# Depthwise 3x3 convolutions from three row-shifted copies in blocks of 32 channels, in place of nine taps on one window

## The chip, the cores and the metric

The kernel runs on one core of a Trainium2 chip. The metric is device time in microseconds (us), the median of several runs; a profile is one further execution, recorded instruction by instruction. The engines are TensorE (PE in the profile, its weight loads PEld), VectorE (DVE), ScalarE (ACT), GpSimd (POOL) and SyncE (SP), which here issues almost all transfers between the memory of the chip (DRAM) and the buffers of the core.

## The reference

Four images of 56 x 56 positions with 96 channels pass through four layers. Layer 0 is a state-space scan in four directions with a feed-forward part; layer 1 has two depthwise convolutions and again a scan in four directions; layers 2 and 3 are linear attention with a quantised feed-forward part. The change touches the convolutions of layer 1 alone:

```python
def _dwconv3(x, w, b):
    y = jax.lax.conv_general_dilated(x, w, (1, 1), [(1, 1), (1, 1)], feature_group_count=x.shape[1], ...)
    return y + b[None, :, None, None]
...
c = jax.nn.relu(_bn(_dwconv3(xc, dw_w, dw_b), ...))        # 96 channels
c = jnp.einsum('bchw,oc->bohw', c, pw_w) + pw_b[None, :, None, None]
conv_out = jnp.transpose(_bn(c, ...), (0, 2, 3, 1))
xz = _ln(x, ln_g, ln_b) @ in_proj_w.T
xm, z = jnp.split(xz, 2, axis=-1)
xm = jax.nn.silu(_dwconv3(xm, conv_w, conv_b))             # 192 channels
...                                                        # the scan of xm in four directions -> y
fused = jnp.concatenate([conv_out, (_ln(y, ...) * silu(z)) @ out_proj_w.T], axis=-1) @ fus_w.T + fus_b
return x + _ln(fused, ...)
```

Each channel has its own 3 x 3 weights, and the image has a border of zeros.

## The kernel before

Channels lie on partitions, positions along the free dimension. An image (L = 3136 positions) is cut into NCW = 7 chunks of CW = 448 positions, which are CR = 8 rows of HS = 56. All is in float32 but for the attention layers' feed-forward part.

**The scan** (`scans`) is the backbone. Its 8 passes (two layers, four images) have 224 rounds each: 4 directions, 7 chunks, NE = 2 halves of 96 channels and NQ = 4 groups of states. In a round VectorE makes two products with `b` (line 695, `b` being a product of TensorE, line 597) and runs three scans (line 702), which need `da` from ScalarE (line 654); GpSimd makes the third product from `cb` (line 690) and multiplies the states by `cb` (line 744), and TensorE adds up the result in four blocks of 32 columns (`add_up`, line 775). `keep_busy` fills TensorE with products with zeros (line 762), as many as a number WARM = 6.8 exceeds the work planned for the round, in which a planned unit counts PER_P = 1.6. The inputs `dt`, `du` and `cb` are loaded through SP's queue by `prepare` (lines 514 and 533), one to four rounds before they are used.

**The lanes** are all the other work: generators `load`, `middle`, `fuse` and `attend`, one of each for each image. Pass p of the scan runs beside `load(1..3)` (p = 0), beside `middle(p - 1)` (p = 1 to 4), and beside `fuse(p - 5)` and `attend(p - 5)` (p = 5 to 7); `fuse(3)` and `attend(3)` begin in pass 7, a chunk as soon as its last direction is summed. What is left when the scans are done runs in `alone` after `late`, with more buffers and no pacing.

A lane runs its seven chunks through `overlap`, up to three at a time (`depth`, 2 for `convolve`, 6 after `late`). A chunk is a generator that yields a slot before each step: the letter is the half of a round ("C" or "F"), the digit the PSUM banks that it holds, `a` and `p` the planned time on ScalarE and TensorE. `room` lets a step run only if the backlog with it stays below ACT_LIMIT = 4.0 and PE_LIMIT = 7.0; `half_round` takes 0.9 and 2.4 from the backlogs twice in a round, and the scan's own work is charged to them too (line 720). The instructions of TensorE, VectorE, ScalarE and GpSimd follow this order exactly; SP issues transfers in the order of the program and stops at one whose buffer is still in use.

**The convolutions.** In `middle(i)`, layer 1's projection writes `md` to DRAM. `convolve` then loads for each chunk two windows (128 and 64 channels) of up to 10 rows with `window` (line 930) into a ring of NWIN = 3 buffers, and `conv` runs nine products with diagonal matrices (line 919), one for each tap, in three steps of three taps. The second part has 64 rows and 64 columns and is split into two halves of four rows. A tap at the image's border covers fewer rows. `diagonals` builds the matrices on GpSimd (line 901), 18 for `middle` and 9 for `fuse`, once each. In `fuse(i)` the same runs on x with 96 channels; the window is kept to the end of the chunk, where line 1162 adds its middle rows to the result. `attend` follows, with two layers of a feed-forward part (`ffn`); line 1189 runs once for each of its chunks, and line 1232 or 1242 stores the chunk.

Of the kernel before, what the change touches and what calls it, by code (L numbers as in the profile page):

```python
# [11 lines left out]
F32 = mybir.dt.float32  # L12
F16 = mybir.dt.float16
BF16 = mybir.dt.bfloat16
F8 = mybir.dt.float8e5
AF = mybir.ActivationFunctionType
ALU = mybir.AluOpType
# [3 lines left out]
HS = 56  # L21
L = HS * HS
C = 96
DI = 192
NS = 16
NE = 2
NG = 3
NQ = 4
NT = 112
CW = 448  # L30
CR = CW // HS
# [5 lines left out]
NCS = L // CS  # L37
RANK = (12, 6)
NW, LATE_NW = 13, 20
NWIN = 3  # L40
OWN = ()
OWN_TAIL = ()

# [2 lines left out]
BANKS, LATE_BANKS = 2, 4  # L46
DEPTH, LATE_DEPTH = 3, 6
# [40 lines left out]
def lay_out(i):  # L88
    i = {k: np.asarray(v) for k, v in i.items()}
    c96, c128, w96, w128, q96, q128 = Cols(C), Cols(128), Cols(C), Cols(128), Cols(C), Cols(128)  # L90
    p0, p1 = "L0_conv_", "L1_conv_"
# [3 lines left out]
    for n in (  # L95
        "dw_b bn1_g bn1_b bn1_m bn1_v pw_b bn2_g bn2_b bn2_m bn2_v ln_g ln_b fus_b fus_ln_g fus_ln_b"
    ).split():
        c96.add("1" + n, i[p1 + n][:, None])
    c96.add("1dw_w", i[p1 + "dw_w"].reshape(C, 9))
    for l in "23":  # L100
        c96.add(l + "bq", i[f"L{l}_attn_bqkv"][:C, None])
        c96.add(l + "bff", i[f"L{l}_attn_bff"][:, None])
# [14 lines left out]
    for l, (xw, dw, db, al, dd) in enumerate(scan):  # L117
        r = RANK[l]
        for k in range(4):
            t = xw[k].T  # L120
            m = np.zeros((128, NE, 2, 64), np.float32)
# [7 lines left out]
            a = al[k].reshape(NE, NG, 32, 4, NQ).transpose(3, 2, 0, 4, 1).reshape(128, -1)  # L129
# [3 lines left out]
    c128.add("0b1", i[p0 + "ffn_b1"].reshape(3, 128).T)  # L133
    for n, v in (
        ("1conv_b", i[p1 + "conv_b"][:, None]),
        ("1conv_w", i[p1 + "conv_w"].reshape(DI, 9)),
        ("1g", i[p1 + "out_norm_g"][:, None]),
        ("1b", i[p1 + "out_norm_b"][:, None]),
    ):
        c128.add(n + "a", v[:128])  # L140
        c128.add(n + "b", v[128:])
# [5 lines left out]
    f = i[p1 + "fus_w"].T  # L147
# [3 lines left out]
    w = i[p0 + "out_w"].T  # L151
# [15 lines left out]
class Net:  # L167
    def __init__(self, ctx, tc, aps, at, out):
        self.tc, self.nc, self.aps, self.at, self.out = tc, tc.nc, aps, at, out
        pool = lambda name, **kw: ctx.enter_context(tc.tile_pool(name=name, **kw))  # L170
        self.const = pool("const", bufs=1)
        self.big = pool("big", bufs=1)
        self.psum = pool("psum", bufs=1, space=bass.MemoryType.PSUM)
        self.dram = pool("dram", bufs=1, space=bass.MemoryType.DRAM)
        self.nw, self.nwin, self.depth, self.banks, self.ring = NW, NWIN, DEPTH, BANKS, None
        self.setup()
        self.dg = None
        self.kept = (0, 0, 0)
        self.ready = set()
        self.live, self.g = [], {}  # L180
        self.backlog, self.paced = [0.0, 0.0], False
        self.work, self.tables = 0.0, False
        self.both = self.big.tile([C, NE, L], F32, name="U")
        self.U = [self.both[:, e] for e in range(NE)]
        self.Y = [self.big.tile([C, L], F32, name=f"Y{e}") for e in range(NE)]
        self.wp = pool("work", bufs=2)
        self.scan_pool = ExitStack()
        self.sp = self.scan_pool.enter_context(tc.tile_pool(name="scan", bufs=2))
        self.pool = pool
        d = lambda name, *shape: [self.dram.tile(list(shape), F32, name=f"{name}{i}") for i in range(NB)]  # L190
        self.xd, self.xrd = d("x", C, L), d("xr", C, L)
        self.ud, self.zd, self.yd, self.md = d("u", DI, L), d("z", DI, L), d("y", DI, L), d("m", DI, L)

    def late(self):

        self.scan_pool.close()
        self.wp = self.pool("late", bufs=2)
        self.nw, self.nwin, self.depth, self.banks = LATE_NW, LATE_DEPTH, LATE_DEPTH, LATE_BANKS
        tags = (("ps", BANKS), ("da0", 1), ("da1", 1), ("da2", 1), ("pp", 1), ("b", 1), ("y", 1))
        self.ring = cycle([t for t in tags for _ in range(t[1])])  # L200

# [8 lines left out]
    def par(self, group, name):  # L210
        a, n = self.at[group][name]
        return self.tiles[group][:, a : a + n]
# [37 lines left out]
    def setup(self):  # L250
        nc, tc, const = self.nc, self.tc, self.const
        par = self.par
# [93 lines left out]
        with tc.tile_pool(name="stage", bufs=1) as st:  # L346
# [10 lines left out]
            self.some = self.upper(self.tiles["w128"][:, :CS])  # L357
            self.minus = const.tile([128, 64], BF16, name="minus")
            nc.vector.tensor_scalar(self.minus[64:], self.ident[64:, 64:], -1.0, None, ALU.mult)
            self.zeros = const.tile([128, C], BF16, name="zeros")  # L360
            nc.vector.memset(self.zeros, 0.0)
            t = st.tile([C, 2, 3, 128], F32, name="q96")
            nc.scalar.dma_start(t.rearrange("p l m f -> p (l m f)"), self.aps["q96"])
# [395 lines left out]

    def add_zeros(self, n):  # L760
        for _ in range(n):
            self.nc.tensor.matmul(self.y[:C], self.zeros, self.some, start=False, stop=False)  # L762

    def add_up(self, ch, e, q, hc):

# [124 lines left out]
        self.nc.sync.dma_start(t, d[:, s])  # L890
        return t

    def diagonals(self, *weights):

        t = self.wp.tile([128, 9, 192], F32, name="dg", bufs=1)
        out, n = [], 0
        for w in weights:
            p = w.shape[0]
            d = t[:p, :, n : n + p]
            for tap in range(9):  # L900
                self.nc.gpsimd.tensor_scalar_mul(d[:, tap], self.ident[:p, :p], w[:, tap : tap + 1])
                yield "F0"
            out.append(d)
            n += p
        return out

    def conv(self, diag, win, lo, *parts):

        taps = [4, 0, 1, 2, 3, 5, 6, 7, 8]
        for n, tap in enumerate(taps):
            dy, dx = tap // 3 - 1, tap % 3 - 1
            x0, x1 = max(0, -dx), min(HS, HS - dx)
            for ps, r0, rows in parts:
                o = ps.rearrange("p (a b) -> p a b", b=HS)
                a, e = max(r0, -dy), min(r0 + rows, HS - dy)
                self.nc.tensor.matmul(  # L919
                    o[:, a - r0 : e - r0, x0:x1], diag[:, tap], win[:, a + dy - lo : e + dy - lo, x0 + dx : x1 + dx],  # L920
                    start=n == 0, stop=n == 8,
                )
            if n in (2, 5):
                yield f"C1 p{3.8 / len(parts)}"

    def window(self, d, rows, c):

        lo, hi = max(0, CR * c - 1), min(HS, CR * c + CR + 1)
        t = self.wp.tile([128, CR + 2, HS], F32, name="win", bufs=self.nwin)[:rows]
        self.nc.sync.dma_start(  # L930
            t[:, : hi - lo].rearrange("p a b -> p (a b)"), d[:, lo * HS : hi * HS]
        )
        return t, lo

    def overlap(self, part, n, depth=9, ready=lambda c: True):

# [66 lines left out]
    def middle(self, i):  # L1003

        nc = self.nc
        par = self.par
        w2 = par("w128", "0w2").rearrange("p (m c) -> p m c", m=3)

# [41 lines left out]
        yield from self.overlap(part, NCW)  # L1050

        if self.dg is None:
            self.dg = yield from self.run(self.diagonals(par("c128", "1conv_wa"), par("c128", "1conv_wb")[:64]))
        dga, dgb = self.dg

        def convolve(c):
            s = slice(c * CW, (c + 1) * CW)
            wa, lo = self.window(self.md[i][:128], 128, c)
            wb, _ = self.window(self.md[i][128:], 64, c)
            yield "C0"  # L1060
            yield "C1 p3.8"
            ps = self.ps()[:, :CW]
            yield from self.conv(dga, wa, lo, (ps, c * CR, CR))
            yield "F0 a3.2"
            t = self.w()
            nc.scalar.activation(t, ps, AF.Silu, bias=par("c128", "1conv_ba"))
            self.exp_and_ln()
            yield "C1 p1.9"
            ps = self.ps()
            o = [ps[64 * h : 64 * h + 64, : CW // 2] for h in range(2)]  # L1070
            yield from self.conv(dgb, wb, lo, *[(o[h], c * CR + h * CR // 2, CR // 2) for h in range(2)])
            nc.sync.dma_start(self.ud[i][:128, s], t)
            yield "F0 a3.4"
            t = self.w(64)
            for h in range(2):
                nc.scalar.activation(
                    t[:, h * CW // 2 : (h + 1) * CW // 2], o[h], AF.Silu, bias=par("c128", "1conv_bb")[:64]
                )
            self.exp_and_ln()
            yield "C0"  # L1080
            nc.sync.dma_start(self.ud[i][128:, s], t)
# [16 lines left out]
    def fuse(self, i):  # L1098

        nc = self.nc  # L1100
        par = self.par
        if len(self.dg) > 1:
            self.dg = yield from self.run(self.diagonals(par("c96", "1dw_w")))
        (dgx,) = self.dg

        def part(c):
            s = slice(c * CW, (c + 1) * CW)
            d, z = self.yd[i], self.zd[i]
            za, zb = self.get(z[:128], 128, s), self.get(z[128:], 64, s)
            win, lo = self.window(self.xd[i], C, c)  # L1110
            yield "C0"
            yield "C1 p3.8"
            ps = self.ps()[:C, :CW]
            yield from self.conv(dgx, win, lo, (ps, c * CR, CR))
            ya, yb = self.get(d[:128], 128, s), self.get(d[128:], 64, s)
            yield "F0 a.7"
            fo = self.w(C)
# [38 lines left out]
            f = yield from self.spread_factor(1e-5, (sq, self.avg96[:, :1]))  # L1156
            yield "C1"
            nc.vector.tensor_tensor(fo, fo, f, ALU.mult)
            yield "C0"
            x = self.w(C)  # L1160
            r = c * CR - lo
            nc.gpsimd.tensor_tensor(x, fo, win[:, r : r + CR].rearrange("p a b -> p (a b)"), ALU.add)
            yield "F0 a.5"
            nc.scalar.activation(x, x, AF.Identity, bias=par("c96", "1fus_ln_b"))
            yield "C1 p1.3"
# [206 lines left out]
```

## Time and profile before

| | |
|---|---|
| median of 3 runs | 8356.53 us (8340.41 to 8364.75) |
| the profiled execution | 8364.46 us, its span 8362.7 us |
| mean granted clock of TensorE | 0.898 |
| busy: PE, DVE, POOL, ACT | 7469.6, 7516.6, 7177.3, 6109.8 us |
| weight loads of TensorE (beside its products) | 2721.6 us |
| DMA: bytes, mean rate | 1417.77 MB, 170 GB/s |
| window loads: count, KB, us to landing | 84 in all; for example 20 of 280 KB, 5.1 us |

A row of the costliest groups reads: line, engine, operation, output and inputs with their shape, count; after the first bar the busy time and the mean duration in ns of one; after the second the idle time of the engine just before them, and what ended most of it. A row of the waits reads: who waited, for what, us in total, times, longest. Busy time is summed over stages with different limits, so what counts is which wait ends last in a stage.

### The profile page before, as it was taken

The page shows a single profiled execution, that of the slowest core. Times are in us where ns is not written, and L with a number is a line of the kernel's source. Part 1 is how long each engine was busy: PE and PEld are TensorE (multiplying, and loading weights), DVE is VectorE, ACT ScalarE, POOL GpSimd, SP SyncE. Part 2 cuts the span into 40 slices and gives each one's busy share as a digit, 9 for nine tenths or more (in the row PEclk, how much of TensorE's full clock was granted, in tenths as well). Part 3 has the DMA queues.
Part 4 walks back from the last instruction along what each step waited for, and adds up shares of the span by engine and source line. Part 5 has one row for each costly group of instructions (what it writes and reads, how often), then busy time and mean ns, then how long its engine had stood idle before and what let it go on. Part 6 is the DMA issues. An engine that isn't in the chain of part 4 may idle for free. (4 is left out here: it accounts for less than half of the span.)

```text
span 8362.7 us, 119228 instructions
## 1 busy us (share of the span) xinstructions
PE 7469.6 (89%) x33633; PEld 2721.6 (33%) x33633; DVE 7516.6 (90%) x9555; ACT 6109.8 (73%) x12807; POOL 7177.3 (86%) x3991
## 2 busy tenths in 40 slices
PE   7889888898889988898899979988899888998997
PEld 3333233232333223232322323333333333333344
DVE  5999999999998999999998999999999999999921
ACT  5778878776787768786777766777776777767736
POOL 4999989989998999899898998998888888889820
PEclk8899989899999989998898989988899888999986
DMA  5777777678766777677776777676766667666721
GB/s 154 179 188 189 203 179 182 167 175 199 178 174 170 172 188 181 172 177 184 177 175 167 174 185 176 166 170 172 186 166 162 166 173 182 167 160 167 175 57 48
DMA packets 944159, 1417.77 MB, mean 170 GB/s; under 512 B 169410, under 2 KB 936644, under 8 KB 942628
## 3 DMA queue, kind: packets, MB, share of 16 engines
q1 hardware_dynamic: 942720, 1408.34, 68.2%
q8 instruction: 264, 4.33, 0.2%
q14 instruction: 403, 3.30, 0.1%
q10 hardware_dynamic: 772, 1.80, 0.1%
HBM read 1141.42 MB, written 268.14 MB: 169 GB/s over the span
## 5 line engine op out<-in xcount | busy, mean ns | idle before, releaser
L702 DVE TENSOR_TENSOR_SCAN h<-da,h 128x449 f32<-128x449 f32 (+1 forms) x5376 | 5507.1, 1071 | 134.9 <-ACT da L654 79.3
L744 POOL TENSOR_TENSOR hc<-h,cb 128x1344 f32<-128x1344 f32 x1792 | 4884.8, 2726 | 598.8 <-DVE h L702 413.6
L654 ACT ACTIVATE da<-dt,na 128x448 f32<-128x448 f32 x5376 | 3353.1, 632 | 1143.2 <-DVE h L702 1104.4
L695 DVE TENSOR_TENSOR h<-du,b 128x448 f32<-128x448 f32 x3584 | 2019.6, 604 | 182.7 <-PE b L597 112.6
L775 PE MATMUL y<-hc,four 128*32 128x448 f32 x14336 | 1913.0, 609 | 17.8 <-POOL hc L744 17.4
L690 POOL TENSOR_TENSOR h<-du,cb 128x448 f32<-128x448 f32 x1792 | 1754.1, 979 | 141.4 <-DMA cb<-cd 110.1
L762 PE MATMUL y<-w,zeros 128*96 128x448 bf16 x4843 | 1354.0, 397 | 0.0
L597 PE MATMUL b<-cf,sel 128*128 128x448 bf16 x1792 | 680.2, 380 | 631.2 <-DVE h L695 626.6
L762 PEld LDWEIGHTS <-zeros 128*96 128x96 bf16 x4843 | 603.2, 135 | 1111.0 <-issue 965.1
L775 PEld LDWEIGHTS y<-hc,four 128*32 128x32 f32 x14336 | 294.2, 113 | 1182.5 <-issue 660.5
L433 PE MATMUL pp<-U,wd 96*128 96x448 f32 x896 | 664.5, 830 | 12.1 <-DMA U<-u 8.3
L771 PE MATMUL y<-Y,ident 96*96 96x448 f32 x672 | 542.9, 898 | 18.6 <-ACT Y L782 14.3
L919 PE MATMUL ps<-win,dg 64*64 64x220 f32 (+11 forms) x1998 | 547.3, 471 | 0.0
L479 PE MATMUL pp<-cf,wd 12*96 12x448 f32 (+1 forms) x896 | 476.2, 613 | 71.7 <-ACT dtc L489 47.6
L672 ACT COPY carry<-h 128x3 f32<-128x3 f32 x1536 | 301.9, 197 | 282.3 <-DVE h L702 276.2
L504 POOL TENSOR_TENSOR duc<-dtc,U 96x896 f32<-96x896 f32 x224 | 483.1, 2157 | 3.3 <-ACT dtc L491 3.3
L782 ACT COPY Y<-y 96x448 f32<-96x448 f32 x448 | 341.7, 763 | 77.7 <-PE y L775 76.8
L919 PEld LDWEIGHTS ps<-win,dg 64*64 64x64 f32 (+2 forms) x1998 | 239.7, 162 | 321.5 <-issue 289.0
L667 ACT COPY h<-carry 128x3 f32<-128x3 f32 x1536 | 280.2, 182 | 66.3 <-POOL hc L744 63.5
L489 ACT ACTIVATE dtc<-pp,wd 96x448 f32<-96x448 f32 x448 | 281.7, 629 | 31.3 <-PE pp L479 27.4
L597 PEld LDWEIGHTS <-sel 128*128 128x128 bf16 x1792 | 183.8, 103 | 336.1 <-issue 272.7
L827 PEld LDWEIGHTS ps<-avg,w 96*112 96x112 f32 (+2 forms) x1944 | 249.9, 193 | 108.1 <-issue 59.0
(427 smaller groups left out, 5933.9 us busy)
## 6 DMA issues: line engine op xcount, KB each, us to landing
cb<-cd SPq DMA_DIRECT2D x3584, 112.0 KB, 3.9
dt<-dd SPq DMA_DIRECT2D x1792, 168.0 KB, 4.3
du<-dd SPq DMA_DIRECT2D x1792, 168.0 KB, 4.1
dd<-dtc SPq DMA_DIRECT2D x224, 336.0 KB, 3.0
dd<-duc SPq DMA_DIRECT2D x224, 336.0 KB, 3.1
U<-u SPq DMA_DIRECT2D x112, 168.0 KB, 4.7
z<-w SPq DMA_DIRECT2D x56, 224.0 KB, 4.5
u<-w SPq DMA_DIRECT2D x56, 224.0 KB, 3.9
```

What stands on the lines that cost most here:

```text
L433: self.nc.tensor.matmul(ch.ps.rearrange("p (a b) -> p a b", b=HS), ch.par.wx[:, e], self.in_order(self.U[e], ch.orient, ch.c * CS, CS), st ...
L504: self.nc.gpsimd.tensor_tensor(in_rows(ch.duc), in_rows(ch.dtc), u[:, :, lo : lo + CS // HS], ALU.mult)
L597: self.nc.tensor.matmul(ps, self.sel[:, q], self.upper(ch.cf), start=True, stop=True)
L654: nc.scalar.activation(da[g][:, INNER], ch.dt[e][:, g], AF.Exp, scale=ch.par.na[:, e, q, g : g + 1])
L690: nc.gpsimd.tensor_tensor(tokens(hs[n])[:, 2], ch.du[e][:, 2], ch.cb[q][:, 1], ALU.mult)
L695: nc.vector.tensor_tensor(tokens(hs[n])[:, g], ch.du[e][:, g], bs[n], ALU.mult)
L702: nc.vector.tensor_tensor_scan(h[:, way], da[g][:, way], h[:, way], 0.0, ALU.mult, ALU.add)
L744: nc.gpsimd.tensor_tensor(hc, tokens(hs[n]), ch.cb[q][:, 0].unsqueeze(1).to_broadcast([128, NG, CS]), ALU.mult,)
L762: self.nc.tensor.matmul(self.y[:C], self.zeros, self.some, start=False, stop=False)
L771: nc.tensor.matmul(o, w, self.in_order(a, ch.orient, ch.c * CS, CS), start=True, stop=False)
L775: nc.tensor.matmul(self.y[32 * n : 32 * n + 32], self.four, hc[:, g], start=n == 3, stop=n == 3 or q == NQ - 1,)
L919: self.nc.tensor.matmul(o[:, a - r0 : e - r0, x0:x1], diag[:, tap], win[:, a + dy - lo : e + dy - lo, x0 + dx : x1 + dx], start=n == 0, st ...
```

## The change

A window now holds three copies of the same rows, shifted by one image row: partitions 0 to 31 the row above, 32 to 63 the row itself, 64 to 95 the row below, for a block of 32 channels. A product with a matrix of 96 rows and 32 columns (three diagonals of 32, one below the other) adds up the three taps of a column of the 3 x 3 weights, so three products make a block's convolution. Two blocks share a window buffer, so 192 channels are six blocks in three buffers, 96 channels three blocks in two. The four blocks of a chunk write to four groups of 32 PSUM partitions, and the order goes over blocks within a tap column. The steps of three taps become one step.

What moves with it: the rows at the image's border need zeros, so the DRAM tensors `x` and `m` get a row of zeros at each end (`xw`, `mw`; `xd`, `md` become views of their inside), written by six transfers at the start of each `middle`. A window takes three loads instead of one, `convolve` loads its third window when it issues the first convolution, and `fuse` loads x again for the last addition in place of reading the window's middle rows. NWIN goes from 3 to 5 and late from 6 to 7. The weights are laid out by row of taps (`by_row`), and the 27 diagonals have 32 columns. The planned work of a convolution goes from three steps of 3.8 to one of 4 and, for the second part, from three of 1.9 to one of 2.

```diff
-NWIN = 3
+NWIN = 5
...
+    by_row = lambda w: w.reshape(-1, 32, 3, 3).transpose(2, 1, 0, 3).reshape(C, -1)
+    c96.add("1dw_w", by_row(i[p1 + "dw_w"]))
+    c96.add("1conv_w", by_row(i[p1 + "conv_w"]))
...
+        self.xw, self.mw = d("x", C, L + 2 * HS), d("m", DI, L + 2 * HS)
+        self.xd, self.md = [[t[:, HS : HS + L] for t in a] for a in (self.xw, self.mw)]
...
-        self.nw, self.nwin, self.depth, self.banks = LATE_NW, LATE_DEPTH, LATE_DEPTH, LATE_BANKS
+        self.nw, self.nwin, self.depth, self.banks = LATE_NW, LATE_DEPTH + 1, LATE_DEPTH, LATE_BANKS
...
-    def conv(self, diag, win, lo, *parts):
-        taps = [4, 0, 1, 2, 3, 5, 6, 7, 8]
-        for n, tap in enumerate(taps):
-            dy, dx = tap // 3 - 1, tap % 3 - 1
+    def conv(self, diag, parts):
+        for n, x in enumerate((1, 0, 2)):
+            dx = x - 1
             x0, x1 = max(0, -dx), min(HS, HS - dx)
-            for ps, r0, rows in parts:
+            for block, win, ps, r0, rows in parts:
                 o = ps.rearrange("p (a b) -> p a b", b=HS)
-                a, e = max(r0, -dy), min(r0 + rows, HS - dy)
                 self.nc.tensor.matmul(
-                    o[:, a - r0 : e - r0, x0:x1], diag[:, tap], win[:, a + dy - lo : e + dy - lo, x0 + dx : x1 + dx],
-                    start=n == 0, stop=n == 8,
+                    o[:, :, x0:x1], diag[block][:, x], win[:, block % 2, r0 : r0 + rows, x0 + dx : x1 + dx],
+                    start=n == 0, stop=n == 2,
                 )
-            if n in (2, 5):
-                yield f"C1 p{3.8 / len(parts)}"
...
-    def window(self, d, rows, c):
-        lo, hi = max(0, CR * c - 1), min(HS, CR * c + CR + 1)
-        t = self.wp.tile([128, CR + 2, HS], F32, name="win", bufs=self.nwin)[:rows]
-        self.nc.sync.dma_start(
-            t[:, : hi - lo].rearrange("p a b -> p (a b)"), d[:, lo * HS : hi * HS]
-        )
-        return t, lo
+    def window(self, d, block, c, n=2):
+        t = self.wp.tile([C, 2, CR, HS], F32, name="win", bufs=self.nwin)
+        rows = d[32 * block : 32 * block + 32 * n].rearrange("(b r) t -> r b t", r=32)
+        for y in range(3):
+            a = (c * CR + y) * HS
+            self.nc.sync.dma_start(
+                t[32 * y : 32 * y + 32, :n].rearrange("p b u v -> p b (u v)"), rows[:, :, a : a + CW]
+            )
+        return t
...
     def middle(self, i):
+        blank = self.zeros.bitcast(F32)
+        for d in (self.xw[i], self.mw[i][:C], self.mw[i][C:]):
+            for a in (0, HS + L):
+                nc.sync.dma_start(d[:, a : a + HS], blank[:C])
...
         def convolve(c):
             s = slice(c * CW, (c + 1) * CW)
-            wa, lo = self.window(self.md[i][:128], 128, c)
-            wb, _ = self.window(self.md[i][128:], 64, c)
+            wins = [self.window(self.mw[i], n, c) for n in (0, 2)]
             yield "C0"
-            yield "C1 p3.8"
+            yield "C1 p4"
             ps = self.ps()[:, :CW]
-            yield from self.conv(dga, wa, lo, (ps, c * CR, CR))
+            self.conv(dg, [(n, wins[n // 2], ps[32 * n : 32 * n + 32], 0, CR) for n in range(4)])
+            win = self.window(self.mw[i], 4, c)
             yield "F0 a3.2"
...
-            yield "C1 p1.9"
+            yield "C1 p2"
             ps = self.ps()
             o = [ps[64 * h : 64 * h + 64, : CW // 2] for h in range(2)]
-            yield from self.conv(dgb, wb, lo, *[(o[h], c * CR + h * CR // 2, CR // 2) for h in range(2)])
+            self.conv(
+                dg,
+                [(4 + n, win, o[h][32 * n : 32 * n + 32], h * CR // 2, CR // 2) for h in range(2) for n in range(2)],
+            )
...
     def fuse(self, i):
-            win, lo = self.window(self.xd[i], C, c)
+            wins = [self.window(self.xw[i], n, c, min(2, NG - n)) for n in (0, 2)]
             yield "C0"
-            yield "C1 p3.8"
+            yield "C1 p4"
             ps = self.ps()[:C, :CW]
-            yield from self.conv(dgx, win, lo, (ps, c * CR, CR))
+            self.conv(dg, [(n, wins[n // 2], ps[32 * n : 32 * n + 32], 0, CR) for n in range(NG)])
...
+            x = self.get(self.xd[i], C, s)
             yield "C0"
-            x = self.w(C)
-            r = c * CR - lo
-            nc.gpsimd.tensor_tensor(x, fo, win[:, r : r + CR].rearrange("p a b -> p (a b)"), ALU.add)
+            nc.gpsimd.tensor_tensor(x, fo, x, ALU.add)
```

## What I predict, and why

> **What bounds the kernel now.** I read the page first: the span is 8362.7 us, and the run that was profiled took 8364.46 us, 8 us above the median of the three timed runs (8356.53). Then the costliest groups:
>
> ```profile
> L702 DVE TENSOR_TENSOR_SCAN h<-da,h 128x449 f32<-128x449 f32 (+1 forms) x5376 | 5507.1, 1071 | 134.9 <-ACT da L654 79.3
> L695 DVE TENSOR_TENSOR h<-du,b 128x448 f32<-128x448 f32 x3584 | 2019.6, 604 | 182.7 <-PE b L597 112.6
> L775 PE MATMUL y<-hc,four 128*32 128x448 f32 x14336 | 1913.0, 609 | 17.8 <-POOL hc L744 17.4
> L762 PE MATMUL y<-w,zeros 128*96 128x448 bf16 x4843 | 1354.0, 397 | 0.0
> L919 PE MATMUL ps<-win,dg 64*64 64x220 f32 (+11 forms) x1998 | 547.3, 471 | 0.0
> ```
>
> VectorE's scans and products sum to 7526.7 us: the 1792 rounds of the scan are VectorE's, until its last scan starts at 7982.8 (the records of line 702). The convolutions' products (line 919) are TensorE's, which has so much spare time that 4843 products with zeros fill it. So their 554 us (18 records more stand under b) are not the path; what they hold up is. I looked for that in the waits, stage by stage. In the stage from 3480 to 3560, where image 2's first depthwise convolution begins, three answers (VectorE, GpSimd, SP's queue) each have one long wait:
>
> ```profile
> DVE h L702 <- POOL h L690: 12.1, 2, 10.1
> POOL h L690 <- DMA cb<-cd: 13.3, 1, 13.3
> SPq L930 <- PE b L597: 15.6, 1, 15.6
> ```
>
> The same place for image 1, in order of time: SP's queue first, then the other engines (start, duration, engine).
>
> ```profile
> 2541.01 0.94 SPq L930 DMA_DIRECT2D win<-m  x2
> 2544.49 0.42 SPq L930 DMA_DIRECT2D win<-m  x1
> 2545.82 1.73 SPq L514 DMA_DIRECT2D du<-dd  x4
> 2560.92 0.47 SPq L930 DMA_DIRECT2D win<-m  x1
> 2563.53 1.78 SPq L533 DMA_DIRECT2D cb<-cd  x4
> ```
>
> ```profile
> 2558.39 2.50 PE L919 MATMUL ps<-win,dg 128*128 128x440 f32 x6
> ...
> 2568.87 0.98 POOL L690 TENSOR_TENSOR h<-du,cb 128x448 f32<-128x448 f32 x1 [12.72 <-DMA cb<-cd]
> 2569.81 2.72 POOL L744 TENSOR_TENSOR hc<-h,cb 128x1344 f32<-128x1344 f32 x1
> 2569.89 1.09 DVE L702 TENSOR_TENSOR_SCAN h<-da,h 128x449 f32<-128x449 f32 x1 [9.56 <-POOL h L690]
> ```
>
> There are three window buffers, and two chunks in flight want four. The fourth load stands in SP's queue until the first chunk's ninth tap (2560.89) frees a buffer; the scan's loads (dt, cb) stand behind it. SP is held 13.7 us and VectorE loses 9.6. All four images have this: SP 12.0, 13.7, 15.6, 14.4 us; VectorE 6.5, 9.6, 10.1, 10.1, and 5.9 in shorter waits for line 690 close by (1.9, 2.0, 2.0): 42 us.
>
> The second place is the end, in two stretches (columns: time, then PE, PEld, DVE, ACT, POOL busy with counts, clock, DMA share, GB/s):
>
> ```profile
> 7985.00:8110.00 125.00, 124.43 (x535) 67.10 (x534) 15.13 (x28) 40.92 (x95) 7.85 (x7) 0.88 0.15 40
> 8110.00:8362.70 252.70, 196.50 (x877) 124.61 (x875) 37.75 (x74) 159.16 (x365) 22.12 (x22) 0.69 0.18 50
> ```
>
> No scan is left there. For 125 us TensorE has no gap: image 3's `fuse`, in which line 919 still has 70 records (3.9 chunks of 18). Then 253 us of feed-forward chunks: line 1189 runs 21 times after 8120, so image 2's second layer (7 chunks) runs there too, 12.0 us a chunk.
>
> **The Trainium skill.** "DMA: Bandwidth & Descriptors", section "Anatomy of one DMA", says that a semaphore wait takes place on the issuing sequencer, not in the DMA engine; so a load without a buffer stops what is queued behind it. The 13.7 us above are that. "TensorE: Matmul & The Clock Gate", Part 3, measures 2.38x for three products of 32 columns side by side; this trace agrees with the kind: line 775's eight records of 609 ns take 0.96 us together, 16 of them 1.71 (at 7986.20). "TensorEngine Tiling (Array Packing)", Key Properties, says that a change of tiling mode drains the array; the trace shows 0.65 to 0.73 us ahead of the first weight load where the form changes.
>
> **The change, part by part.**
>
> *Products.* Before, a `convolve` chunk has 9 products of 128 columns and 18 of 64; line 919 is busy 82.2 us for seven chunks in 2540 to 2800, 11.7 us each. A `fuse` chunk is 18 records at 0.37 us warm (six take 2.46 to 2.50 us, with a drain), about 7.4 us, and 4.77 us for six at a low clock. After, 12 products (24 records) of 96x32 in four column blocks, with line 775's form and 96 rows for 128: three groups of four at 0.8 us, 2.5 us; the second part, of half the length, 1.2 to 2.5, I take 1.8. `fuse`: three groups of three, 2.4 us. So 28 x (4.3 + 2.4) = 188 us for 554: -366 us of TensorE. But `keep_busy` puts zeros back: planned work falls from 17.1 to 6 and from 11.4 to 4 units a chunk, at 1.6 zeros a unit 17.8 and 11.8, times 28 = 829, at 0.28 us (1354.0/4843) up to 232 us. TensorE stays full; beside the scan this is nearly worth nothing. What it brings is fewer late `b`: VectorE waits 31.4 us for line 597 in the four convolve stages (8.9, 3.5, 4.4, 14.6) of 1030 us, 81 us in the other 7300, a rate that would give 11. I take 12 of the other 20; bounds 0 and 25.
>
> *Windows.* Five buffers, two windows of a chunk at its start, the third only when its first convolution is issued. The first two chunks take four buffers at once; the sixth window needs buffer one, whose reader comes a round earlier in the order. The wait of 12 to 16 us goes: -38 us, bounds -42 and, if a shorter wait stays in its place, -15. What is late next is the usual 4 us for `u` on SP (line 1081), which costs VectorE nothing now. In `fuse` three chunks in flight want six of five buffers, once at each image's start: SP can stand up to about 6 us behind the first convolution, against a slack that I read as 4 us (held 13.7, lost 9.6); +2 us times three images.
>
> *Loads.* A window is three loads of 32 rows x 2 x 1792 B, the shape of cb<-cd (112 KB, 0.45 us to issue, 3.9 us to land). `convolve` has nine for two a chunk, `fuse` six and one for x, for one: 28 x 13 = 364 more issues, 164 us of SP. In 2540 to 2800 SP waits 65.5 us on line 508 for dtc and duc, so 7 x 7 x 0.45 = 22 us fit. Bytes: 28 x (1.03 - 0.43 + 0.69 - 0.22) MB = 30 MB on 1418. In the convolve stage that is 0.6 MB in 37 us, 16 GB/s on 174, from a DMA share of 0.70 to 0.77; 600 to 800 had 0.79 with VectorE 99% busy. I charge 10 us; bounds 0 and 224 (below, rival 2). The six edge loads of an image (96 rows of 224 B) are 2 us of SP, hidden.
>
> *Rest.* The 27 diagonals on POOL become narrower (14.1 us, off the path, to perhaps 8). x is now loaded a step ahead of POOL's addition: a round of 4.4 us beside the scan covers 4 us of landing; if not, POOL waits, and `hc` behind it, and the sums behind that. At the end it may show: +3 us.
>
> *Lanes, hence the end.* `overlap` admits work by a budget. A half round returns 2.4 TensorE units, 38.4 per eight rounds; the scan spends 3.4 and 6 or 12 of these, so 2.9 to 3.6 a round are left, mean 3.25. A `fuse` chunk costs 40.1 units, 12.3 rounds (image 0: four convolutions from 5000 to 5200, about as slow); without 7.4 of them 10.1. At 4.39 us a round (7870/1792) that is 9.8 us a chunk, 69 us an image. Pass 7 (6975 to 7985) inherits image 1's feed-forward until 7260 and has all of `fuse(2)`; `attend(2)`'s first layer ends only near 8002. About 80 units fall away in pass 7, and what image 1 gives back comes on top. The second layer of image 2 is bound by ScalarE, so I let only 70 us of progress count, at 37 us a chunk two chunks of 12.0 us: -24, and half a chunk of `fuse(3)` that ends inside the scan, at 125/4 us: -15. The convolutions left in the stretch to 8110: 3.9 chunks cost 18 records x 0.37 to 0.74, about 36 us; after, 3.4 x 3 = 10, but at a clock that sinks when TensorE empties, so -20 of these 26. Sum for the end: -24 - 15 - 20 + 3 = -56; bounds -20 and -95.
>
> **Sum.** -12 - 38 + 6 + 10 - 56 = -90 us on 8364 gives 8274; the profiled run stood 8 us above the median, so against the median 8266.
>
> **Rivals.**
> 1. *Only the stall goes.* The zeros take TensorE's time, the granted clock at the end falls from 0.88, and ScalarE bounds image 2's chunks: the end keeps its 377 us but for 15. Then -38 + 16 - 15 = -37: 8320. For it: only line 1189's 21 chunks and their 0.69 clock decide the last 253 us. Against: 125 us of gapless TensorE.
> 2. *SP's queue becomes the bound (slower).* Place: the start of each chunk of `convolve` and `fuse`, where six loads (2.7 us) and then three more stand ahead of dt, du and cb, and x waits for a `w` buffer. From about 4 us of lateness on, each further one is VectorE's. At 4 us lost in each of 56 chunks: +224 - 90 = +134, 8490. For it: line 690 waits up to 18.6 us for cb in this trace. Against: SP's spare 65 us per stage, and L508's waits, which absorb a burst every chunk.
> 3. *The blocks don't run side by side.* 24 records one after another are 8.9 us in one place, planned as 4: VectorE waits some 4 us for `b` in 56 places, +224 less 50: 8530. Against it: line 775.
> 4. *Nothing that can be measured*: small losses of SP eat the gain, 8345.
>
> **Numbers.** A run of this kernel can tell 0.3%, 25 us, from no change. Forecast 0.60 (8225 to 8315), more than that 0.07, rival 1 0.12, rival 4 0.09, rival 2 0.09, rival 3 0.03. Faster by over 0.3%: 0.60 + 0.07 + 0.10 = 0.77; same 0.11; slower 0.12. The range reaches up over rival 4 and down to the end's bound of -95 with the full -42: 8200 to 8365.
>
> **What would show it.** The waits of SP for a free window (line 930) of 12 us or more, and the four waits of VectorE near 10 us, are gone; convolution records near 1850 but busy under 250 us; zeros up to 5700; the last scan near 7950; after it fewer than 21 runs of what is line 1189 now. I am wrong if cb or du waits appear all through the convolve and fuse stages (rival 2), if records of a group start one after another (rival 3), or if the stretch after the last scan stays at 377 us (rival 1).

## The result, and the profile after

The changed kernel takes 8312.01 us (median of 5 runs, 8308.29 to 8323.64) against 8356.53 (5 runs, 8340.41 to 8365.89): a ratio of 0.9952, with a 95% interval of 0.9936 to 0.9968, so 44.5 us less. That lies inside the range and has the sign of the forecast, but is half its size. The profiled execution of the changed kernel took 8309.25 us, its span is 8307.5, so the two profiles differ by 55 us.

From the page of the changed kernel: the row of the DMA packets, three of the costliest rows (the lines 702, 695 and 762 of before, now shifted by two), and the window loads of `m`.

```profile
DMA packets 971491, 1448.97 MB, mean 174 GB/s; under 512 B 177922, under 2 KB 969732, under 8 KB 969956
...
L704 DVE TENSOR_TENSOR_SCAN h<-da,h 128x449 f32<-128x449 f32 (+1 forms) x5376 | 5505.2, 1070 | 102.5 <-ACT da L656 75.6
...
L697 DVE TENSOR_TENSOR h<-du,b 128x448 f32<-128x448 f32 x3584 | 2015.3, 602 | 188.2 <-PE b L599 107.5
...
L764 PE MATMUL y<-w,zeros 128*96 128x448 bf16 x5188 | 1450.6, 399 | 0.0
...
win<-m SPq DMA_DIRECT2D x252, 112.0 KB, 3.6
```

The bytes grew by 31 MB, as worked out. The products with zeros grew by 345 and by 97 us. VectorE's idle time before a scan fell from 134.9 to 102.5 us, but before its products with `b` it did not fall (182.7, now 188.2). The convolutions are gone from the costliest rows: in the stage of image 1's `convolve` (time; busy of PE and PEld with counts, clock, DMA share, GB/s, line 916 alone) they take 30.2 us for seven chunks, 4.3 each.

```profile
2530.00:2800.00 270.00, 30.17 (x336) 11.57 (x336) 0.89 0.76 188
```

The waits of VectorE over the whole run (who waited, for what; us in total, times, longest):

```profile
DVE h L697 <- PE b L599: 107.5, 94, 10.5
...
DVE w L1137 <- ACT w L816: 47.2, 17, 8.8
...
DVE h L704 <- POOL h L692: 24.0, 22, 2.0
```

The long wait for line 690, now 692, is gone: its longest is 2.0 us, where images 1 to 3 had one each of 9.6 to 10.1 (the 6.5 of image 0 was a wait for `du`, and is gone too). In its place the wait for `b` has one of 10.5 us. Where that one stands, first SP's queue and then the other engines show, in order of time (start, duration, engine; in brackets the wait ahead of it):

```profile
2525.03 2.92 SPq L927 DMA_DIRECT2D win<-m  x6
...
2530.35 3.59 SPq L927 DMA_DIRECT2D win<-m  x6
2534.05 1.78 SPq L516 DMA_DIRECT2D du<-dd  x4
2535.93 1.79 SPq L516 DMA_DIRECT2D dt<-dd  x4
2537.82 1.78 SPq L535 DMA_DIRECT2D cb<-cd  x4
2539.96 1.88 SPq L927 DMA_DIRECT2D win<-m  x3
```

```profile
2533.47 2.44 PE L916 MATMUL ps<-win,dg 96*32 96x448 f32 x24
...
2545.79 6.59 PE L916 MATMUL ps<-win,dg 96*32 96x224 f32 x48 [6.17 <-DMA win<-m]
2552.31 0.37 PE L599 MATMUL b<-cf,sel 128*128 128x448 bf16 x1
...
2580.08 3.56 PE L916 MATMUL ps<-win,dg 96*32 96x224 f32 x48
```

```profile
2552.79 1.15 DVE L697 TENSOR_TENSOR h<-du,b 128x448 f32<-128x448 f32 x2 [10.49 <-PE b L599]
```

The first convolution runs at 2533.47. The third window's loads follow it in the program, but SP is busy with the second chunk's six loads and twelve of the scan's, and issues them at 2539.96. The second part's products stand next in TensorE's order, with the second chunk's first part, 48 records together; they wait 6.2 us for the window, and then take 6.59 us where the next such 48 take 3.56 (at 2580.08). `b` stands behind them. VectorE loses 10.5 us, at the place where it lost 9.6 before. Images 2 and 3 have the same wait, of 8.6 and 10.0 us; image 0 has none. So of four waits behind a transfer queue, three came back behind TensorE's. A second profile of the same kernel has the same three (10.6, 10.5 and 10.1 us), and 122.0 us of waits for `b` in all.

The end, in the two stretches that answer to those of before:

```profile
7975.00:8085.00 110.00, 102.86 (x339) 45.27 (x335) 10.64 (x18) 32.25 (x67) 7.25 (x6) 0.66 0.22 62
8085.00:8307.50 222.50, 174.71 (x850) 116.93 (x849) 33.79 (x66) 132.10 (x305) 18.65 (x18) 0.71 0.17 47
```

`fuse(3)` takes 110 us for 125, the feed-forward chunks 222 for 253, and line 1192 (1189 before) runs 16 times there instead of 21. The granted clock of the first stretch is 0.66, where it was 0.88.

By the scan's passes (from the start of each pass's first scan; all such figures below are worked out from the starts in the trace in this way), where the time went:

| us | pass 0 | passes 1 to 4 | passes 5 to 7 | after the last scan |
|---|---|---|---|---|
| before | 934.1 | 3913.4 | 3022.4 | 379.9 |
| after | 935.5 | 3873.3 | 3049.7 | 332.5 |
| after, profiled once more | 934.5 | 3888.4 | 3065.5 | 320.0 |

The two profiles of the same program differ by up to 16 us in a column, so a smaller difference between two single profiles shows nothing by itself. Passes 1 to 4, beside `middle`, gained 25 to 40 us, the end 47 to 60, and passes 5 to 7, beside `fuse` and `attend`, lost 27 to 43.

### The profile page after: what moved, and what is told of

Its sections match the earlier page's. It is cut to its first block, busy times and chain, and to the rows that moved or that the text cites. A ratio compares the mean times of both kernels' runs of the same rounds, so it can differ in the third digit from the quotient of the medians.

```text
span 8307.5 us, 120108 instructions
## 1 busy us (share of the span) xinstructions
PE 7301.1 (88%) x33810; PEld 2600.4 (31%) x33810; DVE 7505.9 (90%) x9555; ACT 6109.7 (74%) x12807; POOL 7170.8 (86%) x3991
## 4 chain that ended last, share of the span: by engine, by line
PE 31%; DVE 25%; ACT 13%; issue 11%; POOL 8%; DMA 8%; SPq 2%; DVEq 0%; POOLq 0%; ACTq 0%
DVE h L704 19%; PE y L777 6%; DVE h L697 6%; POOL hc L746 5%; PE y L764 4%; ACT da L656 4%; DMA cb<-cd 3%; PE y L773 3%; PE b L599 2%; DMA du<-dd 2%; PE pp L481 2%; PE ps L844 2%; POOL h L692 2%; PE ps L829 1%; ACT L808 1%
## 5 line engine op out<-in xcount | busy, mean ns | idle before, releaser
L704 DVE TENSOR_TENSOR_SCAN h<-da,h 128x449 f32<-128x449 f32 (+1 forms) x5376 | 5505.2, 1070 | 102.5 <-ACT da L656 75.6
L697 DVE TENSOR_TENSOR h<-du,b 128x448 f32<-128x448 f32 x3584 | 2015.3, 602 | 188.2 <-PE b L599 107.5
L777 PE MATMUL y<-hc,four 128*32 128x448 f32 x14336 | 1940.5, 617 | 17.1 <-POOL hc L746 16.6
L764 PE MATMUL y<-w,zeros 128*96 128x448 bf16 x5188 | 1450.6, 399 | 0.0
L764 PEld LDWEIGHTS <-zeros 128*96 128x96 bf16 x5188 | 645.5, 135 | 1188.4 <-issue 1029.2
L570 ACT COPY cf<-pp 64x448 f32<-64x448 f32 x448 | 235.6, 526 | 88.4 <-PE pp L592 80.2
L829 PEld LDWEIGHTS ps<-avg,w 96*112 96x112 f32 (+1 forms) x1984 | 254.8, 193 | 99.7 <-issue 57.5
L844 PEld LDWEIGHTS ps<-ident,rs 112*96 112x96 f32 x1784 | 223.4, 188 | 131.2 <-issue 87.9
```

Source lines behind the costliest of these rows:

```text
L697: nc.vector.tensor_tensor(tokens(hs[n])[:, g], ch.du[e][:, g], bs[n], ALU.mult)
L704: nc.vector.tensor_tensor_scan(h[:, way], da[g][:, way], h[:, way], 0.0, ALU.mult, ALU.add)
L764: self.nc.tensor.matmul(self.y[:C], self.zeros[:, :C], self.some, start=False, stop=False)
L777: nc.tensor.matmul(self.y[32 * n : 32 * n + 32], self.four, hc[:, g], start=n == 3, stop=n == 3 or q == NQ - 1,)
```

## The experiments

Three things ask for a test: whether the buffer's wait was worth 38 us, whether the third window took some of it back, and why the passes 5 to 7 became slower. Each kernel's time stands as a ratio to that of the kernel before on the same chip. In what follows "the plan" is the planned TensorE time by which `room` admits the lanes' steps.

**One buffer more, nothing else.** The kernel before with its ring of windows one longer.

```diff
-NWIN = 3
+NWIN = 4
```

> The kernel before with four window buffers in place of three, nothing else. Theory S: SP is no longer held 12 to 16 us at the first convolution of each image, VectorE's four waits of 6.5 to 10.1 us and what follows them go, 8315 to 8325 us, all of it in passes 1 to 4. Rival (something else comes late in the same place, a load or TensorE): less than 15 us of gain, 8341 us or more.

Measured: 0.9958 (0.9941 to 0.9975), 8313.71 us. Before and this run, the same three waits:

```profile
DVE h L695 <- PE b L597: 112.6, 143, 4.6
POOL h L690 <- DMA cb<-cd: 110.1, 28, 18.6
...
DVE h L702 <- POOL h L690: 53.2, 26, 10.1
```

```profile
DVE h L695 <- PE b L597: 106.2, 136, 5.4
...
POOL h L690 <- DMA cb<-cd: 60.1, 25, 18.7
...
DVE h L702 <- POOL h L690: 17.6, 20, 2.4
```

VectorE's wait for line 690 falls by 35.6 us, GpSimd's for `cb` by 50, and passes 1 to 4 by 42.3 (3871.1); the other columns are as before (3023.3 and 379.9). The forecast's -38 for the wait holds, and a single digit gives as much as the whole change.

**The third window with the other two.** The changed kernel with all three windows asked for at a chunk's start, in six buffers.

```diff
-NWIN = 5
+NWIN = 6
-            wins = [self.window(self.mw[i], n, c) for n in (0, 2)]
+            wins = [self.window(self.mw[i], n, c) for n in (0, 2, 4)]
...
-            win = self.window(self.mw[i], 4, c)
+            win = wins[2]
```

The ring after `late` goes back from seven to six.

> The changed kernel, with the third window of a convolve chunk loaded beside the other two at the chunk's start (six buffers in place of five, six in place of seven at the end). Theory S (the wait for a buffer on SP's queue came back as a wait of TensorE for the third window, because that is asked for only one step before it is used): the three waits of VectorE for b of 8.6 to 10.5 us in images 1 to 3 go, passes 1 to 4 become some 25 us shorter, 8287 us. Rival (the burst of nine loads at once delays the scan's own loads): the waits come back as waits for cb or du, 8312 us or more.

Measured: 0.9925 (0.9906 to 0.9944), 8296.53 us. TensorE no longer waits for a window of `m` at all (17.1 us before), and the longest wait for `b` is 4.6 us:

```profile
DVE h L697 <- PE b L599: 93.1, 91, 4.6
```

Passes 1 to 4 take 3861.1 us, 12 and 27 less than the two profiles of the changed kernel; the ratios differ by 22 and 30 us, and the intervals of the first pair touch. So the late third window cost some 20 us of the 29 that its three waits show, as an estimate. The loss in passes 5 to 7 (3054.7) stays.

**The change with the old plan.** The products stay, but go out in three steps again, one tap column each, each charged as the old steps were (3.8, and 1.9 for the second part).

```diff
+            if n < 2:
+                yield f"C1 p{cost}"
...
-            yield "C1 p4"
+            yield "C1 p3.8"
...
-            yield "C1 p2"
+            yield "C1 p1.9"
```

> The changed kernel with the convolutions planned as before: three steps, one tap column each, charged 3.8 (and 1.9) units. The products, windows and loads are the new ones. Theory L (the gain at the end and the loss in passes 5 to 7 both come from the plan: lanes that are charged less run ahead and denser): the stretch after the last scan goes back from 332 us to 360 or more, and passes 5 to 7 get back some 20 of the 27 us that they lost; the total stays within 15 us of 8312. Rival P (it is the shorter products themselves that shorten the end): the stretch stays near 335 us, and the total is 8312 or less.

Measured: 0.9891 (0.9874 to 0.9909), 8259.75 us, 51 us below the changed kernel by the ratios. The end goes back as theory L has it, to 369.8 us; but passes 5 to 7 get back more than all they lost (3008.9), and passes 1 to 4 gain too (3827.9), which neither forecast had. VectorE's waits for `b` are nearly halved:

```profile
DVE h L697 <- PE b L599: 60.6, 63, 3.6
```

So the cheap products are worth much beside the scan, 52 us of waits for `b`, and the change as made doesn't get it. Against the one buffer more alone the ratio is 0.9891/0.9958, which is 56 us less.

**The new plan with the old products.** The reverse: the kernel before, its nine taps in three steps, but the first charged 4 (or 2) and the others nearly nothing.

```diff
             if n in (2, 5):
-                yield f"C1 p{3.8 / len(parts)}"
+                yield "C1 p0.01"
...
-            yield "C1 p3.8"
+            yield "C1 p4"
...
-            yield "C1 p1.9"
+            yield "C1 p2"
```

> The kernel before with nine taps and old windows, but planned like the changed one: the first step of three taps charged 4 (and 2) units, the other two nothing. Theory L: the stretch after the last scan falls from 380 us to about 350, and passes 5 to 7 grow by 25 us or more, since the taps still cost TensorE their time; total 8345 to 8370. Rival P: the end stays at 370 us or more, and the total is above 8360.

Measured: 1.0118 (1.0097 to 1.0138), 8455.32 us, slower than I had expected.

```profile
DVE h L695 <- PE b L597: 182.0, 152, 4.9
```

Passes 1 to 4 lose 60 us (3973.0), passes 5 to 7 71 (3093.6), and the end gains 31 (348.8). These products are dearer than their charge here, so the sizes don't carry over. The pattern does: a lower charge for all convolutions moves work from the end into the scan, and the scan's passes pay more than the end gains.

**Is it the plan, the number of steps, or the burst?** Three kernels with the new products, between the change (one step, low charge) and the one with the old plan (three steps, high charge). First three steps with the low charge: the steps of the third experiment, 4 (or 2) for the first and 0.01 for the other two.

> The changed kernel with the convolution in three steps, one tap column each, but charged as in the change: 4 (and 2) units at the first step, nothing for the other two. Theory C (what the old plan won in the run after_old_pace is the charge: lanes that pay less run too dense for VectorE): the time stays at 8300 to 8320 us, passes 5 to 7 near 3050 us, the end near 332 us. Theory B (it is the size of the burst: 24 records of TensorE in one step come ahead of b): passes 1 to 4 fall from 3873 to some 3830 us, and the time to 8270 us.

Then one step, and the old charge all at once, at its issue:

```diff
-    def conv(self, diag, parts):
+    def conv(self, diag, parts, rest):
+        self.spend(0, rest)
```

with `rest` 7.4, and 3.7 for the second part.

> The changed kernel with the convolution in one step as in the change, but charged as before in all: 7.4 (and 3.7) units more are put on the backlog when it is issued. Theory C: passes 5 to 7 fall from 3050 to some 3010 us, the end rises from 332 to about 370 us, passes 1 to 4 keep only the three waits for the third window (about 3850 us); 8285 us. Theory B: passes 1 to 4 stay at 3873 us, passes 5 to 7 near 3040, and with the longer end the time is above 8320 us.

Then the old three steps with their old charge, but all products in the first; the other two are charged and empty:

```diff
+        for _ in range(2):
+            yield f"C1 p{cost}"
```

> The kernel of after_old_pace with all products of a convolution in the first of its three steps; the other two steps issue nothing but are charged 3.8 (and 1.9) as before. So the plan, the zeros and the lanes' pace are those of after_old_pace and the burst is that of the change. Theory Z (the charge spread over three rounds is what wins, through pace and fewer zeros): 8255 to 8275 us, 4843 products with zeros. Theory B (the burst of 24 records ahead of b loses the rest): 8285 us or more, with waits of VectorE for b near 90 us.

| products in | charge | ratio (95%) | wait for `b`, us (longest) | passes 1 to 4 | passes 5 to 7 | end | zeros |
|---|---|---|---|---|---|---|---|
| one step | low (the change) | 0.9952 (0.9936 to 0.9968) | 107.5 (10.5) | 3873.3 | 3049.7 | 332.5 | 5188 |
| three steps | low | 0.9956 (0.9944 to 0.9968) | 97.9 (5.9) | 3878.4 | 3044.4 | 337.4 | 5214 |
| one step | high, spread over three | 0.9961 (0.9948 to 0.9974) | 95.3 (4.8) | 3859.2 | 3043.8 | 378.4 | 4843 |
| one step | high, at once | 0.9936 (0.9924 to 0.9948) | 65.9 (4.1) | 3855.7 | 3005.8 | 369.0 | 5226 |
| three steps | high, spread | 0.9891 (0.9874 to 0.9909) | 60.6 (3.6) | 3827.9 | 3008.9 | 369.8 | 4843 |

The first two of these kernels came out as theory C has it, the third is as slow as theory B says. Three readings. The end follows the charge alone: 332 to 337 us with the low one, 369 to 378 with the high one. Smaller steps alone bring nothing, nor does the spread charge alone; together they bring 0.6 to 0.7%. And the zeros are not what holds `b` up: the third row has as few as the last and waits as long as the second, the fourth has the most and waits little.

The traces show what the burst costs in passes 1 to 4, if VectorE's waits for `b` are summed over the rounds in which TensorE has a convolution and the round right behind each. They are 39.0 us in the change (29 of them at the third window), 11.7, 10.7 and 12.8 in the next three rows, and 1.7 in the last; the kernel before had 30.7. So small steps with the whole charge take nearly all of them. In passes 5 to 7 it is not the burst: there these waits are 8 to 11 us in the first four rows and 6 in the last, and theory B's 90 us of waits for `b` came out (95.3) with only 19 of them near a convolution. What the first three rows lose in these passes (VectorE is idle for 200 to 204 us, in the last two for 170) is spread over waits for `b` in other rounds and waits for the lanes' results. Its cause stays open, and so does most of the 28 us by which the fourth row's passes 1 to 4 stand above the last row's (11 of them are waits for `b`).

**The loads alone.** The kernel before with four buffers, and beside its windows as many loads of 112 KB (or 56) more as the change issues, 7 in a chunk of `convolve` and 6 in one of `fuse`, into a buffer of their own that nothing reads.

```diff
+            self.more(self.md[i], 4)
             yield "C0"
...
+            self.more(self.md[i], 3)
             yield "F0 a3.2"
...
+            self.more(self.xd[i], 3)
+            self.more(self.xd[i], 2, 1)
             yield "C0"
...
+            self.more(self.xd[i], 1)
```

> The kernel before with four window buffers, and with as many more loads as the change has (seven a convolve chunk, six a fuse chunk, in the change's shape and places, into a buffer that nothing reads; the result doesn't use them). Theory: SP and the DMA engines have room for them, 8314 to 8335 us. Rival (the loads themselves are what passes 5 to 7 of the changed kernel lose): 8350 us or more, with waits for cb and du in all convolve and fuse stages.

Measured: 0.9997 (0.9988 to 1.0006), 8342.46 us. Against the four buffers alone the ratio is 0.9997/0.9958, 0.39% or 33 us, from two chips; the profiles differ by 20 (spans 8342.8 and 8322.9), 11 of them in passes 1 to 4 and 8 at the end, each within the spread of single profiles. The prediction of the change had 10 in all, and neither forecast of this run names the time that came out. The scan's own loads do come later, against 60.1 and 17.6 us in the kernel with four buffers:

```profile
POOL h L690 <- DMA cb<-cd: 91.2, 29, 17.6
...
DVE h L702 <- POOL h L690: 30.8, 29, 2.5
```

So GpSimd waits 31 us longer for `cb`, and 13 us of that reach VectorE. The loss that passes 5 to 7 of the changed kernel show isn't there (3025.5).

**Versions.** Three more look for what is left with the old plan. First `fuse` of images 2 and 3 alone at a low charge (1.33 a step), so that the end gets the shorter plan where it helps:

```diff
-            yield "C1 p4"
+            cost = 3.8 if i < 2 else 1.33
+            yield f"C1 p{cost}"
```

> The kernel of after_old_pace (three steps, charged 3.8 and 1.9) with the convolutions of images 2 and 3 in fuse charged 1.33 a step, so that only pass 7 and the end run with the dense plan. Theory C and L: the end falls from 370 to about 335 us, pass 7 grows by 15 to 25 us, passes 1 to 6 stay; 8240 to 8250 us, faster than the change and the kernel before. Rival (what the end wins, pass 7 loses in full): 8260 us or more.

Measured: 0.9894 (0.9871 to 0.9918), 8251.61 us. The end falls to 327.5, passes 5 to 7 rise by 15 and passes 1 to 4, which run the same program, by 15 too: by its time not to be told from the kernel with the old plan. In the profile the low charge for these two alone takes 42 us from the end for 15 in passes 5 to 7, a better exchange than the change's 37 for 41; the times don't confirm it. Then the old plan with the third window early:

> The kernel of after_old_pace with the third window loaded beside the other two (six buffers). Theory S: with three steps the third window is no longer late, nothing is left to win there, 8250 to 8265 us. Rival: waits for it still hide in the shorter ones, 8245 us or less.

Measured: 0.9912 (0.9895 to 0.9929), no gain. With the convolution in three steps, the request and the second part both stand two rounds later in the program, and TensorE waits for windows of `m` only 2.7 us as it is, so there is nothing to take. Last, the old plan with one load for each row shift, over all six blocks (three loads a chunk for nine, of 336 KB), in two such buffers, four of half the size after `late`:

```diff
-            wins = [self.window(self.mw[i], n, c) for n in (0, 2)]
+            win = self.window(self.mw[i], 0, c, 2 * NG)
```

> The kernel of old_pace_third_early with one load for each row shift over all blocks: three loads of 336 KB in place of nine for a convolve chunk, three of 168 KB in place of six for a fuse chunk, the same bytes (two window buffers of six blocks; four of three blocks at the end). Theory (of the 30 us that the added loads cost in before_4win_loads the number of issues on SP's queue is the larger part): 10 to 20 us less than old_pace_third_early, 8235 to 8250 us. Rival (it is the bytes, or the two buffers hold the third chunk of fuse back): the same or slower, 8255 us or more.

Measured: 0.9936 (0.9918 to 0.9954), slower than with nine loads, by 0.45% against the kernel with the old plan and 0.24% against the one with the early third window, whose interval overlaps: passes 1 to 4 lose 21 us and the end 17 against the former. Whether the two buffers or the larger loads do it, this run doesn't tell.

**The change once more**, on another chip, for the spread:

> The changed kernel once more, unaltered, for the spread of its passes from one profile to the next: 8312 us within 10; each pass within 10 us of its first profile. If the sums of passes 1 to 4 and 5 to 7 move by more than 15 us, differences of that size between single profiles tell nothing.

Measured: 0.9961 (0.9948 to 0.9975), 8319.48 us; its passes are in the first table.

## Why the prediction was wrong by half

*Windows, -38.* Right in its size: the extra buffer alone takes 42 us from passes 1 to 4. Wrong in what comes next. "What is late next is the usual 4 us for `u` on SP (line 1081), which costs VectorE nothing now" overlooked the load that the change itself asks for a step before its use. I had counted its place in SP's queue, but not that the second part's products stand ahead of `b` on TensorE and wait for it. It gives back some 20 us, by the estimate above. The forecast asked of the wait on SP what stands behind it; it didn't ask that of the wait on TensorE.

*Late `b`, -12, bounds 0 and 25.* The mechanism was right and sized too small, for a kernel that was not built. With the old plan the waits for `b` fall by 52 us, and 37 of these stand in the rounds with a convolution or right behind one. In the change they are 107.5 and 122.0 us in two profiles, for 112.6 before: 29 us of the third window are in them, and the burst leaves about 10 more in passes 1 to 4.

*Lanes, hence the end, -56.* The end is 47 and 60 us shorter, so the sum was right, in part by luck. Its parts were not: with the old plan the end is only 10 us shorter, so the shorter products are worth about 10 us there (less than the spread of single profiles), and the rest is work moved into the scan, five chunks of the second layer rather than two. **The step that failed is that I priced the lower charge, and the work that it moves, at nothing beside the scan.** I let "70 us of progress count" and took no time for it beside the scan. Passes 5 to 7, for which the forecast had the 6 of the sixth window and a part of the loads, rose by 27 and 43 us; with the old charge, in three steps or paid at once, they stay at 3006 to 3009, below before. The whole price of the plan as it was changed, charge and steps together, is 49 us in the profiles (51 by the ratios): it takes 45 in passes 1 to 4 (the third window's some 20 among them) and 41 in passes 5 to 7, and gives 37 at the end. The forecast had only the gain.

What the runs show in its place differs by stage. In passes 1 to 4 no work moves (VectorE runs 112 instructions for the lanes before and after), so the low charge and the single step only cost: VectorE's waits for `b` there are 55.2 us in the change and 13.0 with the old plan, 42 of the 45 us (29 of them at the third window). In passes 5 to 7 its instructions for the lanes went from 274 to 294 and from 140.7 to 149.1 us, and its idle time ahead of them from 81.5 to 101.2; ahead of the scan's own it is the same within 3 us (in the second profile, with 43 us lost, 107.7 ahead of the lanes' and 10 more ahead of the scan's). So the 27 us of the first profile are the lanes' work on VectorE and its waits for their results, as the row of line 1137 shows (26.5 us before, 47.2 after). How much of this is the moved work alone stays open: with the products in one step and the high charge spread over three, nothing moves (274 instructions, an end of 378 us), and passes 5 to 7 take 3043.8 us all the same.

*Loads, +10, bounds 0 and 224.* Too small: 20 to 33 us. The bounds hold. Rival 2 (SP becomes the bound) does not hold in its size, but its mechanism is there in small: with the loads alone, VectorE loses 13 us to late `cb`.

*Products.* Right: a group of four blocks runs side by side, 24 records in 2.44 us, so rival 3 falls, and a `convolve` chunk takes 4.3 us as forecast (its second part is 1.33 us when alone and at speed). The number of records is 1848. The zeros came to 5188, not up to 5700. One sum was misread, without effect on the forecast: 7526.7 us for VectorE's scans and products counts the overlap of neighbouring records twice, since all of VectorE is busy for 7516.6 us.

*Fuse's sixth window, +6.* No wait of SP for a window's reader of over 0.5 us shows in the trace, so nothing speaks for it. The reloaded x makes GpSimd wait 12.6 us in five places.

Rivals 1 and 4, 8320 and 8345, stand nearer to the result than the forecast, but for other reasons than theirs: the end did become shorter (though the granted clock in its first stretch fell, as rival 1 had it), and most of the loss came from TensorE's order and the plan, not from SP. That the result lies in the stated range says little, since the range was drawn to reach over rival 4.

## What to carry to other kernels

A wait taken out of one in-order queue is only gone if what the change asks for instead is early by the queue's own length. Follow the new request to the engine that consumes it, and see what stands behind the consumer. Where side work is admitted by planned costs, these are a throttle and not a description: change the work and the charge separately, because a truer (lower) charge can cost more beside the bound engine than it saves later (with three steps, 0.9956 against 0.9891). And ask for the smallest edit that removes the wait: here one more buffer gave as much as the whole change (0.9958 and 0.9952), and the new products with the old charge gave 0.9891, the best of all with 8259.75 us (the variant with a quicker end, 0.9894 and 8251.61, can't be told from it).

## What the runs showed of the hardware

- TensorE is slower after the wait that it was made to take. The 48 records behind the window's wait of image 1 last 0.62 us each in the median and up to 0.96, and end after 6.59 us; the same 48 at 2580.08 last 0.45 and end after 3.56. The granted clock was 0.53 in the first stretch and 1.00 in the second. Images 2 and 3 show it too: after waits of 5.56 and 5.33 us the 48 records take 5.28 and 6.87 us, at clocks of 0.67 and 0.50. So in image 1 the 6.2 us of waiting became 9.2 us of lateness for `b`.
- 364 loads more, 2.7% of the bytes, cost 20 to 33 us, though SP had 65 us of waiting in a convolve stage and a load is 0.45 us to issue. GpSimd's waits for `cb` grew by 31 us and VectorE's for GpSimd by 13; no wait shows the rest.
- The new products run side by side: 24 records of 96 rows, 32 columns and 448 positions took 2.44 us together, 24 of 224 positions 1.33 us, both at a granted clock of 1.00.
